# Four images through four fused layers: how far layer 0 of the next image runs ahead, and in which pool a second set of tiles lies

## The chip, the cores and the metric

The kernel runs on one core of one Trainium2 chip. Its time is device microseconds of one launch; the median of several runs is the metric. PE is TensorE, DVE is VectorE, ACT is ScalarE, POOL is GpSimd, SP is the engine that issues most DMAs. Each engine takes its instructions in the order of its own queue; semaphores order them across engines.

## The reference

Four images of 32×32 pixels and 384 channels in float32 go through four residual layers, each on a group-normalized input:

```python
x = x + _L0_conv_ref(_gn(x), ...)   # deformable attention, 6 heads of 64
x = x + _L1_conv_ref(_gn(x), ...)   # attention, 12 heads of 32, weighted by a group similarity
x = x + _L2_conv_ref(_gn(x))        # box sums over 5 pixels and 20 channels, quotient
x = x + _L3_conv_ref(_gn(x), ...)   # 3x3 outlook attention
```

Layer 0 makes queries `q`, a grouped 3×3 convolution of them, LayerNorm, GELU and a tanh offset per pixel and group. At the offset positions it samples the image bilinearly (a gather), makes keys and values from the samples, samples a table of relative biases for each pair of pixels, and takes a softmax over 1024 keys:

```python
attn = jnp.einsum('bmhc,bnhc->bhmn', qh, k) * scale
attn = jax.nn.softmax(attn + bias, axis=-1)
out = jnp.einsum('bhmn,bnhc->bmhc', attn, v)
```

Layer 1 takes `softmax(q k)`, multiplies it by a group weight, and normalizes over the queries (`axis=2`) before it multiplies by the values:

```python
sim = jax.nn.sigmoid(sim_beta + sim_alpha * jnp.einsum('bhnd,bhmd->bhnm', _l2norm(xg_h), _l2norm(gc)))
group_weight = jnp.einsum('bhnm,bhkm->bhnk', sim, sim) * gamma + (1.0 - gamma)
attn = softmax(q k * scale) * group_weight
attn = attn / (attn.sum(axis=2, keepdims=True) + 1e-08)
out = jnp.einsum('bhnm,bhmd->bhnd', attn, v)
```

Images are independent of each other.

## The kernel before

There are two lanes. **Front** does layer 0 of an image; **Trunk** does layers 1, 2 and 3. Layer 0 of image 0 runs by itself first. After that, the trunk of image b has layer 0 of image b+1 beside it, and the trunk of the last image has nothing beside it. The lanes hand over through DRAM: layer 0 writes `x1[b % 2]`, the trunk reads it.

Both lanes are Python generators that yield a weight after each small step. `layer3` draws from them: it advances the trunk by one step, adds the step's weight over `TRUNK_STEPS` (1109) to `done`, and then draws steps of the fronts, each worth its weight over `FRONT_STEPS` (714), until `ahead` has reached `done + LEAD`. So LEAD is the share of an image by which layer 0 of the next images is ahead of even progress. The order of these calls gives the priority; the scheduler of the language then places the instructions on each engine's queue, where an instruction that could be ready earlier may be put ahead of its turn.

The front of one image has these parts, with their steps: in `inputs0`, norm and transposes (35), queries (15, L553), the grouped convolution (45, L572), transposes, LayerNorm (L601 to L623) and GELU (L627) (25), `positions` (20, L433 to L503), eight gathers with their weighing and turning (64, L640, L653 to L656, L667), keys and values (30, dense products L364 and L378, evacuated at L694 and L700); then 12 half-heads of 38 steps in `head0`; then `w_out` (18). A half-head is 512 queries of one head. For each of eight key tiles it gathers a window of the bias table (`win`, L722), interpolates it (`z` L734 and L735, `lg` L739 and L740), multiplies queries and keys (L743), adds (L744) and keeps a running maximum (L749). Then come the maximum's broadcast (L762), the exponentials (L775, L776) and the products with values and ones (L778).

The trunk of one image: `inputs1` (173 steps) has the norm, queries and keys of layer 1 (evacuated at L847 and L849), the gate's projection and its strided depthwise convolution (L881, L883), the inverse norms (`inv`, L912), values (L919), and the normalized gates (L930, L938, L944); the softmax sums of the first four heads go in between (`sums_step`, L1011 to L1024). Then six `pair`s of heads (118 steps each): similarities (`sims`, L1064 and L1071), and for eight key tiles the scaled similarity `sg` (POOL, L1126), logits (L1141), exponent (L1149), similarity product (L1171), the weighting with the sum over queries (L1180) and the products with the values (L1115). Last, `layers23` (228 steps): `out1` (L1219), the box sums (L1235 to L1282), and layer 3 (attention and values L1302 to L1316, convolution of the weights L1341, a skewed copy through DRAM L1375 and L1377, products L1387, output L1401).

Tiles lie in pools that are opened and closed by `scope`, the trunk's from the low end of SBUF, the front's from the high end. In the trunk, pool `l1` is open for the whole layer 1, `l1a` for `inputs1`, `l1b` for the pairs. In the front, `l0` is open for the whole layer, `l0a` for `inputs0`, `l0b` for the heads. `pair_tiles` makes two sets of queries and keys (`qks[0]`, `qks[1]`, two tiles of 4 KB per partition each) in `l1`, and fills their padding rows by memsets on POOL (L966, L967). Pair p uses set p % 2; `load_pair(0)` is called in `inputs1`, `load_pair(1)` in the first pair. By the built program, `l1a` ends at byte 141056 of a partition, and `l0b` begins at byte 140576.

Of the kernel before, what the change touches and what calls it, by code (L numbers as in the profile page):

```python
# [26 lines left out]
P = 128  # L27
NB, HW, C = 4, 32, 384
N = HW * HW
# [3 lines left out]
NH1, HD1 = 12, 32  # L33
# [25 lines left out]

TRUNK_STEPS, FRONT_STEPS, LEAD = 1109.0, 714.0, 0.1


def bc(ap, axis, n):
# [7 lines left out]
class Net:  # L73
# [190 lines left out]
    def layer1(self, b):  # L264
        self.stages = [self.trunk.layer1(b)]
# [547 lines left out]
class Trunk(Lane):  # L813
# [3 lines left out]
    def layer1(self, b):  # L817
        with self.scope("l1"):
            self.pair_tiles()
            with self.scope("l1a"):  # L820
                yield from self.inputs1(b)
            with self.scope("l1b"):
                self.load_groups(0)
                st = None
                for p in range(NH1 // 2):
                    if p % 2 == 0:
                        u = p // 2 + 1
                        st = self.sums_state() if u < NH1 // 4 else None
                        if st:
                            self.load_quad(u)  # L830
                    yield from self.pair(p, st)
# [121 lines left out]
    def pair_tiles(self):  # L953

        nc = self.nc
        self.qks = [[self.wt([P, N], f"{t}{i}") for t in ("qa", "ka")] for i in range(2)]
        self.xg, self.gc = self.wt([P, N], "xg"), self.wt([P, M1], "gc")  # L960

        self.q4, self.k4 = self.wt([P, N], "q4"), self.wt([P, N], "k4")
        for r in range(2):
            rest = slice(64 * r + HD1, 64 * r + 64)
            for qa, ka in self.qks:
                nc.gpsimd.memset(qa[rest, :], 0.0)  # L966
                nc.gpsimd.memset(ka[rest, :], 1.0)  # L967
            nc.gpsimd.memset(self.xg[rest, :], 0.0)
            nc.gpsimd.memset(self.gc[rest, :], 0.0)

    def load_quad(self, u):

        rows = slice(u * P, (u + 1) * P)
        for t, src in ((self.q4, self.qd), (self.k4, self.kd)):
            self.nc.sync.dma_start(t, src[rows, :])
# [512 lines left out]
```

## Time and profile before

| | us |
|---|---|
| median of 3 runs | 5136.31 |
| runs | 5131.72, 5136.31, 5164.89 |
| the profiled execution | 5153.4 |
| its span, first to last instruction | 5151.6 |

| stage, by the trunk's marks in the trace | image 1 | image 3 |
|---|---|---|
| inputs of layer 1 | 1925 to 2145 | 4310 to 4488 |
| six pairs | 2145 to 2885 | 4488 to 4958 |
| layers 2 and 3 | 2885 to 3139 | 4958 to 5151 |

Image 1 has layer 0 of image 2 beside it, image 3 has nothing. Layer 0 of image 0 takes the first 641 us by itself. The mean granted TensorE clock is 0.871. A busy time in a window is the union of the records of an engine[...].

### The profile page before, as it was taken

Reading aid. Unit: us, or ns where it says so; the run is one execution under the profiler, and the core shown is the slowest. Engines: PE = TensorE matmul, PEld = TensorE weight load, DVE = VectorE, ACT = ScalarE, POOL = GpSimd, SP = SyncE. Lnnn points to the kernel's source line nnn. Section 1 sums busy time; section 2 is a strip of 40 time slices with the busy share of each in tenths; the row PEclk is TensorE's granted clock in tenths of the full one; section 3 lists DMA queues with packets and bytes.
Section 4 is the critical chain, followed back from the end, with each engine's and each line's share of the span. In section 5 each row is a group of like instructions: output and inputs, shape, how many; then the busy total and the mean of one; then the engine's idle time right before and its main releaser. Section 6 shows DMA issues by size and latency. Waiting matters only on the chain.

```text
span 5151.6 us, 47071 instructions
## 1 busy us (share of the span) xinstructions
PE 4290.8 (83%) x15676; PEld 1844.1 (36%) x15676; DVE 3213.1 (62%) x5718; ACT 2406.5 (47%) x4346; POOL 1069.2 (21%) x994
## 2 busy tenths in 40 slices
PE   4466687899898788799999889799999978899976
PEld 2122242333343353233333344233334334243434
DVE  3478627577877725567777753667787772455544
ACT  2155424566755113466666312456675511566520
POOL 1523203211212301221222210321121230000011
PEclk7677786899999887799999889689999988799987
DMA  5323242311212142221112124231121213101011
GB/s 113 107 80 87 69 149 73 104 45 46 72 42 83 37 134 93 83 88 56 57 53 60 46 86 138 83 95 51 42 77 42 73 52 108 55 11 31 14 36 37
DMA packets 226578, 361.60 MB, mean 70 GB/s; under 512 B 115939, under 2 KB 163136, under 8 KB 226336
## 3 DMA queue, kind: packets, MB, share of 16 engines
q1 hardware_dynamic: 165448, 192.11, 12.2%
q0 software_dynamic: 39936, 145.53, 9.7%
q10 hardware_dynamic: 20952, 20.96, 1.6%
q8 instruction: 124, 2.03, 0.2%
q14 instruction: 118, 0.97, 0.1%
HBM read 280.59 MB, written 79.26 MB: 70 GB/s over the span
## 4 chain that ended last, share of the span: by engine, by line
PE 52%; DVE 23%; ACT 12%; issue 6%; DMA 4%; POOL 3%; another core or an unknown queue 0%; SPq 0%; ACTq 0%; DVEq 0%; POOLq 0%
PE bank L1171 11%; PE big L364 7%; PE bank L778 5%; PE big L1141 5%; ACT big L1024 4%; PE bank L378 4%; PE bank L743 3%; PE big L1011 3%; DVE nmax L1019 3%; DVE lg L744 2%; DVE e L1180 2%; PE bank L1115 2%; DVE rmax L749 2%; PE bank L318 2%; PE bank L1166 2%
## 5 line engine op out<-in xcount | busy, mean ns | idle before, releaser
L1180 DVE SCALAR_TENSOR_TENSOR e<-bank,gam,e 128x512 f32<-128x512 f32 x768 | 562.8, 748 | 558.5 <-ACT gn L1179 253.0
L1171 PE MATMUL bank<-sim,sg 128*128 128x512 f32 (+3 forms) x2304 | 856.5, 508 | 5.1 <-DVE e L1180 5.1
L1024 ACT ACTIVATE big<-big,nmax 128x512 f32<-128x512 f32 x768 | 508.6, 662 | 421.2 <-DVE nmax L1019 380.2
L722 POOL DMA_INDIRECT win<-strips,widx x384 | 418.4, 1090 | 979.6 <-DVE z L735 414.9
L1149 ACT ACTIVATE e<-big 128x1024 f32<-128x1024 f32 x384 | 378.5, 1021 | 372.4 <-PE big L1141 362.3
L1171 PEld LDWEIGHTS bank<-sim,sg 128*128 128x128 f32 x2304 | 407.3, 199 | 363.0 <-issue 287.1
L1019 DVE TENSOR_REDUCE nmax<-big 128x2 f32<-128x1024 f32 x384 | 459.4, 1219 | 122.1 <-PE big L1011 82.2
L1011 PE MATMUL big<-k,q 32*128 32x512 f32 x1536 | 403.6, 744 | 146.6 <-ACT big L1024 74.4
L1141 PE MATMUL big<-qa,ka 64*128 64x512 f32 x1536 | 418.1, 627 | 16.2 <-ACT big L1024 8.0
L1126 POOL TENSOR_SCALAR sg<-sim,gam 128x512 f32<-128x512 f32 x192 | 152.0, 795 | 1323.7 <-PE bank L1171 963.2
L778 PE MATMUL bank<-lg,va 128*64 128x512 f32 x768 | 382.7, 649 | 41.6 <-ACT lg L776 41.5
L743 PE MATMUL bank<-qpad,kz 128*128 128x512 f32 x768 | 390.7, 639 | 25.2 <-DVE e L1180 13.2
L778 PE MATMUL bank<-lg,ones 128*64 128x512 f32 x768 | 382.0, 648 | 0.0
L734 ACT ACTIVATE z<-win,bias_f 128x528 f32<-128x528 f32 x384 | 277.8, 738 | 202.0 <-DVE lg L740 119.3
L740 DVE SCALAR_TENSOR_TENSOR lg<-z,bias_f,lg 128x512 f32<-128x512 f32 x384 | 290.2, 767 | 64.2 <-ACT lg L739 61.6
L640 POOL DMA_INDIRECT gat<-pairs,sidx x192 | 206.4, 1075 | 583.1 <-DVE ix_fl L451 328.6
L735 DVE SCALAR_TENSOR_TENSOR z<-win,bias_f,z 128x528 f32<-128x528 f32 x384 | 292.9, 777 | 39.0 <-ACT z L734 27.5
L739 ACT ACTIVATE lg<-z,bias_f 128x512 f32<-128x512 f32 x384 | 270.4, 721 | 47.3 <-DVE z L735 34.3
L775 DVE TENSOR_TENSOR lg<-lg,tb 128x512 f32<-128x512 f32 x384 | 240.6, 686 | 77.2 <-ACT tb L768 77.2
L744 DVE TENSOR_TENSOR lg<-bank,lg 128x512 f32<-128x512 f32 x384 | 257.4, 684 | 47.0 <-PE bank L743 44.0
L776 ACT ACTIVATE lg<-lg 128x512 f32<-128x512 f32 x384 | 222.5, 629 | 39.2 <-DVE lg L775 38.8
L743 PEld LDWEIGHTS bank<-qpad,kz 128*128 128x128 f32 x768 | 138.9, 197 | 271.8 <-issue 141.3
(252 smaller groups left out, 6040.8 us busy)
## 6 DMA issues: line engine op xcount, KB each, us to landing
pairs<-xn SPq DMA_DIRECT2D x64, 192.0 KB
w<-in_gmat SPq DMA_DIRECT2D x16, 576.0 KB
w<-in_w_off SPq DMA_DIRECT2D x12, 576.0 KB
w<-in_Wqkv SPq DMA_DIRECT2D x12, 576.0 KB
a<-in_x SPq DMA_DIRECT2D x16, 384.0 KB
x<-a ACTq DMA_DIRECT2D x4, 1536.0 KB
k<-a SPq DMA_DIRECT2D x12, 512.0 KB
kz<-k SPq DMA_DIRECT2D x24, 256.0 KB
```

Source lines behind the costliest of these rows:

```text
L364: nc.tensor.matmul(ps[:, h * 512 : (h + 1) * 512], w[:, ki, lo + ko * P : lo + (ko + 1) * P], mov, start=ki == 0, stop=ki == KC - 1,)
L722: nc.gpsimd.indirect_dma_start(out=win, out_offset=None, in_=self.strips[:, :], in_offset=bass.IndirectOffsetOnAxis(ap=self.widx[:, q, c : ...
L743: nc.tensor.matmul(ps, kz[:, j * P : (j + 1) * P], both, start=True, stop=True)
L744: v.tensor_tensor(lf, ps, lf, ALU.add)
L778: nc.tensor.matmul(po[out, :], w, lf, start=j == 0, stop=j == NJ - 1)
L1011: nc.tensor.matmul(ps[c // 2][:, c % 2, :], self.q4[rows, i * P : (i + 1) * P], self.k4[rows, h * 512 : (h + 1) * 512], start=True, stop=True,
L1019: v.tensor_reduce(nmax[:, 2 * g : 2 * g + 2, i, h], ps[g], AX.X, ALU.max, negate=True)
L1024: nc.scalar.activation(ps[g][:, r, :], ps[g][:, r, :], AF.Exp, bias=nmax[:, c, i, h : h + 1], accum_out=den[:, c, i, h : h + 1],)
L1141: nc.tensor.matmul(ps[:, r, :], ka[rows, j * P : (j + 1) * P], qa[rows, cols], start=True, stop=True,)
L1149: nc.scalar.activation(e, ps, AF.Exp)
L1171: nc.tensor.matmul(ps[:, (mid - i0) * P :], sg[:, r, m, :], sim[:, r, m, mid * P : i1 * P], start=m == 0, stop=m == 1,)
L1180: v.scalar_tensor_tensor(e[:, r, :], ps, self.gam[:, 1:2], e[:, r, :], ALU.add, ALU.mult, accum_out=tot[:, r, h : h + 1],)
```

## The change

LEAD becomes 0.18, which is 57 front steps more. The second set of queries and keys is made at the start of the pairs, in pool `l1b`, and its four memsets are issued there; the first set stays in `l1`. Pool `l1a` then begins 8192 bytes lower and ends at byte 132864; `l1b` keeps its end. Lines after `load_groups(0)` move by 1, those after `pair_tiles` by 8. No arithmetic is added or removed.

```diff
-TRUNK_STEPS, FRONT_STEPS, LEAD = 1109.0, 714.0, 0.1
+TRUNK_STEPS, FRONT_STEPS, LEAD = 1109.0, 714.0, 0.18
...
                 self.load_groups(0)
+                self.pair_set()
                 st = None
...
-        self.qks = [[self.wt([P, N], f"{t}{i}") for t in ("qa", "ka")] for i in range(2)]
+        self.qks = []
+        self.pair_set()
         self.xg, self.gc = self.wt([P, N], "xg"), self.wt([P, M1], "gc")
...
-            for qa, ka in self.qks:
-                nc.gpsimd.memset(qa[rest, :], 0.0)
-                nc.gpsimd.memset(ka[rest, :], 1.0)
             nc.gpsimd.memset(self.xg[rest, :], 0.0)
             nc.gpsimd.memset(self.gc[rest, :], 0.0)
+
+    def pair_set(self):
+
+        qa, ka = [self.wt([P, N], f"{t}{len(self.qks)}") for t in ("qa", "ka")]
+        for r in range(2):
+            rest = slice(64 * r + HD1, 64 * r + 64)
+            self.nc.gpsimd.memset(qa[rest, :], 0.0)
+            self.nc.gpsimd.memset(ka[rest, :], 1.0)
+        self.qks.append((qa, ka))
```

## The prediction

> **What bounds the kernel now.** I first read the busy shares, then cut the span at the trunk's own marks (its first query evacuation, first `sims`, first `out1`) and asked for the busy time of each engine in each piece. Image 1 with layer 0 of image 2 beside it is the first three rows below; image 3, which has nothing beside it, the last three. Columns: stretch, length, busy PE, weight loads, DVE, ACT, POOL, then the granted PE clock, DMA share, GB/s.
>
> ```profile
> PE 4290.8 (83%) x15676; PEld 1844.1 (36%) x15676; DVE 3213.1 (62%) x5718; ACT 2406.5 (47%) x4346; POOL 1069.2 (21%) x994
> ...
> 1925.00:2145.00 220.00, 169.03 (x455) 68.13 (x447) 128.42 (x198) 83.79 (x184) 61.04 (x66) 0.72 0.31 99
> 2145.00:2885.00 740.00, 690.90 (x2675) 280.97 (x2676) 542.05 (x1066) 469.55 (x829) 151.99 (x154) 0.97 0.21 61
> 2885.00:3139.00 254.00, 208.05 (x782) 107.78 (x784) 126.91 (x164) 47.20 (x75) 51.90 (x24) 0.83 0.29 88
> 4310.00:4488.00 178.00, 143.79 (x363) 58.26 (x363) 75.89 (x92) 70.31 (x158) 10.00 (x18) 0.77 0.24 84
> 4488.00:4958.00 470.00, 450.08 (x2029) 194.33 (x2028) 244.93 (x602) 285.53 (x523) 33.20 (x48) 0.99 0.07 21
> 4958.00:5151.00 193.00, 119.37 (x376) 70.57 (x376) 91.85 (x101) 15.88 (x23) 44.38 (x19) 0.74 0.13 40
> ```
>
> The reader is to see three kinds of stage. The pairs (740 us) are TensorE's: 691 of 740 busy at clock 0.97. The inputs of layer 1 (220) are a chain of short waits: PE shows 169 busy, but at 0.72, and DVE 128. The tail, layers 2 and 3 (254), lies between. Beside layer 0 they cost 42, 270 and 61 us more than alone. So the question is which part of layer 0 lies beside which stage. The chain that ended last, cut to the end of the inputs and the start of the pairs (start, length, what):
>
> ```profile
> 2068.64 8.15 DVE inv L912
> ...
> 2097.48 9.24 PE bank L378 x24
> ...
> 2116.23 1.75 DVE gat L653
> ...
> 2136.98 3.79 PE big L930 x4
> ...
> 2176.75 15.45 PE big L364 x36
> 2192.20 15.49 PE bank L378 x48
> 2208.44 4.65 DMA win<-strips,widx
> ```
>
> Two things are to be seen. The end of the inputs waits for DVE, layer 0's weighing (L653) among it; and the keys and values of layer 0 (15.45 + 15.49 = 30.9 us of unbroken PE) stand on the chain inside the pairs, where PE is short, followed by a 4.65 us window gather.
>
> **What the Trainium skill says.** "TensorE: Matmul & The Clock Gate", Part 1, has an idle PE fall to half clock and warm up under load. The trace agrees in kind: 0.72 to 0.77 in the gappy stages, 0.97 to 0.99 in the pairs. So "PE busy" overstates the work in the inputs. The same page (the section on the array of 32×32) calls ACT and DVE strict FIFOs; the trace fits it, since a trunk instruction never passes a front instruction ahead of it. "ScalarE: Activation LUTs", What ACT_TABLE_LOAD costs, gives about 1283 ns for a table load; this trace has 1283 ns for each of its 109.
>
> **The change, part by part.** *The lead.* 0.08 of 714 steps is 57 steps; each stage of the trunk now has a later part of layer 0 beside it. By the built programs' order on each engine:
> - inputs of layer 1: before, third convolution, LayerNorm, GELU, positions, five of eight gathers; after, all eight gathers, keys and values, and 16 `z`, 13 `lg` of head 0.
> - pairs: before, three gathers, keys and values, then 10.5 half-heads; after, 12 half-heads without those first 16 and 13.
> - tail: before, 1.5 half-heads, `w_out`, then norm, transposes, queries, two convolutions; after, `w_out`, then all of that, the third convolution, LayerNorm, GELU and positions.
>
> *Pairs, each of three.* PE at full clock: a half-head is 16 query-key records at 15.45/36 = 0.43 us (6.9), 32 value records (7.0 in the chain's rows of L778) and about 1.7 of transposes and the ones-matmul (estimated from the same 0.43), 15.6 in all. 12 less two tiles is 185; before, 10.5 half-heads and three more query-key tiles, 30.9 and some 2 of turns make 200. So PE gives back 15. DVE: the moved `z` and `lg` (16×0.777 + 13×0.767 = 22.4), keys and values (3×1.28 + 8×0.56 = 8.3) and three weighings (3×3.3) leave, 1.5 half-heads of some 14 each in exponent and maximum work come: about -20. ACT gives back 7, and four of its table loads per image (109 become 93 in all), 5 us. The stage's full-clock PE sum is about 625 by the same rates (an estimate: 200 for layer 0 and 425 for the trunk, which alone shows 450 busy), so 740×15/625 = 18; I take 17. 3×17 = 51.
>
> *Inputs.* PE gains 30.9 and 1.7 of query-key, loses 8 of convolution. DVE loses LayerNorm and positions (16 + 22, as the first image alone spends them between 87.7 and 127.9 us) and gains 10 + 8 + 22: even. The first 110 us of the stage, 91 alone, should save about 10, since weighing (8×3.3 = 26) replaces 39. The end, from L912 on, should lose: the kv block stands on PE ahead of L930, then the first window gather (4.65) and 16 `z` stand on DVE among L938 and L944. It lasts 68 us now, at a PE clock of 0.55 to 0.61 in the windows from 2068 to 2145; I take 83. Sum +5 for images 1 and 2. Image 0, where LayerNorm and positions stand in the opening burst before the trunk's first key evacuation (L849), gets +10: some 15 for the 16 us of LayerNorm less part of the same saving. Together +20. Bounds: -15 per image if kv fits in the idle PE, +30 if all of it is exposed.
>
> *Tail.* PE loses 14, DVE gains 23, but where it is free: after L1316 the trunk uses 6 us of DVE in 54. Convolutions move ahead of L1341 (16 us where there were about 10 of other work: +4), the heads leave the DVE-bound box sums. I take -10 for images 0 and 1, where the bounds are -25 and +15. For image 2 only `w_out` is left beside 213 us that are 193 alone: -9. Sum -29.
>
> *Edges.* The last image alone stays 841 us. Layer 0 of image 0 stays.
>
> *The second set.* Its four memsets (0.945 us each, 3.8) move to the start of the pairs, behind 20 window gathers in POOL's order and ahead of `sg`; its loads stand behind them on SP, and only the next pair needs them. Cover: `load_groups` and `sims` (four ACT evacuations of 1.2). Zero; at worst 4 per image. What it gives: the input pool ended at byte 141056 of a partition, the heads' pool of layer 0 begins at 140576; now it ends at 132864, so heads may start before the inputs end without a wait.
>
> Sum: -51 + 20 - 29 = -60 on the profiled execution's own 5153.4 us, 1.2%. The median of the runs, 5136.31, is 17 lower; the same share of it gives 5136.3×(1 - 60/5153) = 5076.5.
>
> **Rivals.** *No gain:* the kv block and its gather are exposed at the end of each inputs stage, +30 instead of +5 to +10, and the pairs keep their losses at boundaries. -51 + 90 - 29 = +10, near 5146; half of it gives 5111. For: L930 stands behind kv on an in-order PE. Against: at a clock of 0.55 to 0.61 PE is far from full in those 68 us. *Slower:* LayerNorm of the next image holds the trunk's outputs. All eight L1401 stand behind L623 on DVE, with positions' four 3.35 us instructions between them. If layer 0's convolutions come late, 16 + 5 (GELU) + 22 us fall in the path at both boundaries, and after the burst once more before L849: 3×43 = 129; with the forecast's -60, and 20 off that its sum already holds for image 0 and the convolutions, +49: 5185. It decides from the point at which L601 starts more than some 15 us after L1316's last. Against: the trunk waits there 11 us for its skewed rows' DMA anyway. *Not as it says:* no stage gains from its new neighbour, and only the loss of overlap is left. 640 (layer 0 alone) + 841 - 1214 = 267 us are saved per overlapped image; 0.08 of it is 21 us lost at the edges. That is contained in the edges above, and alone gives 5157.
>
> **How the numbers follow.** Forecast 0.55, no gain 0.22, loss of overlap only 0.08, slower 0.15. The forecast's own range is 5015 to 5110: three inputs at -15 to +15, tails at -25 to 0. Within 1% is about what a measurement of this kernel can tell from no change: below 5085 counts as faster. The forecast lies mostly there, so faster 0.54; same 0.3; slower 0.16. The range for 8 in 10 is 5015 to 5170, leaving the larger half of the slower case out.
>
> **What would show it.** Right: pairs with layer 0 beside them at 720 to 726, inputs at 220 to 235 with more PE and a higher clock, tails 240 to 250, last image 841. Wrong: L930 waiting for L364 or `win` for over 20 us, L1401 ending later after L1316, `sg` waiting for the memsets of `qa`, or pairs that stay at 740, which would say that PE's sum is not what sets them.

## The result, and the profile after

The changed kernel takes 5153.93 us in the median of 10 runs (5144.38 to 5157.43). The kernel before, beside it on the same chip, takes 5141.27 in the median of 10. The ratio is 1.0019, 95% interval 1.0004 to 1.0033: no difference of 1% in either direction, where a gain of 1.2% was forecast. The profiled run took 5157.4 us with a span of 5155.6.

The gain was made and given back within each image. The table cuts both profiled executions at the trunk's own marks: from the last output of the image before to the first query evacuation ("gap", for image 0 the opening norm), from there to the end of `inv`, from there to the start of the first evacuation of `sims`, then the pairs, up to the evacuation of the sixth one's output, and the tail. Microseconds, before → after:

| | gap | to `inv` | end of inputs | pairs | tail | sum |
|---|---|---|---|---|---|---|
| image 0 | 92 → 96 | 119 → 139 | 70 → 93 | 739 → 728 | 257 → 233 | 1277 → 1289 |
| image 1 | 34 → 43 | 119 → 107 | 72 → 95 | 736 → 730 | 254 → 234 | 1215 → 1209 |
| image 2 | 34 → 39 | 119 → 107 | 71 → 94 | 734 → 727 | 213 → 199 | 1171 → 1166 |
| image 3 | 30 → 30 | 100 → 100 | 53 → 53 | 466 → 465 | 191 → 192 | 840 → 840 |

Stages with the same work in them differ by up to 5 us within one execution (67, 70 and 72 us for the end of the inputs in the kernel with seven parts and lead 0.10, below), so a single difference of that size says little.

The page's busy line of the kernel after, and its table by windows. The columns are stretch, length, busy PE, weight loads, DVE, ACT, POOL, granted PE clock, DMA share and GB/s. The first row is image 0 up to `inv`; the others are image 1, stage by stage.

```profile
PE 4253.8 (83%) x15676; PEld 1825.4 (35%) x15676; DVE 3239.3 (63%) x5718; ACT 2383.3 (46%) x4330; POOL 1082.6 (21%) x994
...
743.00:883.00 140.00, 95.76 (x242) 37.32 (x241) 98.91 (x143) 52.48 (x107) 51.98 (x48) 0.72 0.30 97
...
1937.00:1980.00 43.00, 15.87 (x47) 11.26 (x48) 17.72 (x61) 1.62 (x3) 24.17 (x32) 0.52 0.35 110
1980.00:2087.00 107.00, 93.24 (x242) 36.41 (x241) 69.70 (x73) 46.59 (x97) 35.48 (x30) 0.79 0.32 104
2087.00:2182.00 95.00, 81.71 (x193) 33.56 (x192) 53.21 (x70) 45.18 (x99) 23.09 (x22) 0.74 0.47 153
2182.00:2912.00 730.00, 680.05 (x2669) 268.43 (x2667) 536.62 (x1056) 459.50 (x816) 137.32 (x139) 0.98 0.18 50
2912.00:3146.00 234.00, 183.13 (x772) 100.39 (x772) 129.53 (x170) 40.30 (x69) 48.77 (x22) 0.85 0.33 98
```

The same cuts in the kernel before, at the marks of the table: image 0 to `inv`, image 1 to `inv`, the end of image 1's inputs, and its pairs.

```profile
738.00:857.00 119.00, 91.73 (x239) 35.11 (x237) 79.51 (x137) 52.24 (x108) 17.87 (x18) 0.80 0.26 86
...
1958.00:2077.00 119.00, 90.84 (x239) 35.13 (x237) 80.08 (x138) 52.27 (x108) 17.22 (x18) 0.81 0.26 86
2077.00:2149.00 72.00, 52.85 (x118) 20.07 (x118) 44.53 (x47) 30.26 (x75) 33.81 (x30) 0.59 0.38 121
2149.00:2885.00 736.00, 690.62 (x2674) 280.87 (x2675) 538.78 (x1063) 468.00 (x827) 151.99 (x154) 0.97 0.21 62
```

Three things are to be seen. The end of the inputs has 28.9 us more of PE in it (52.85 to 81.71, 75 more matmul records) and is 23 us longer. In the pairs PE lost 10.6 us against image 1 of before (690.6 to 680.1), and the stage only 6. And image 0 up to `inv` has 19 us more of DVE and 34 more of POOL than before, where image 1 has 10 less of DVE.

What stands on the path at the end of the inputs is in the chain of waits after, image 2 from `inv` to the first `sims` (start, length, what):

```profile
3283.89 8.15 DVE inv L913
...
3296.27 15.72 PE big L364 x36
3311.99 12.27 PE bank L378 x38
...
3324.99 4.93 DMA win<-strips,widx
...
3330.25 0.75 ACT z L734
...
3331.02 0.78 DVE z L735
...
3354.86 3.81 DMA win<-strips,widx
...
3374.72 3.78 PE big L931 x4
3378.50 3.71 PE big L1072 x6
```

The keys and values of layer 0 (L364, L378) are an unbroken 28 us of PE that begins 4 us after `inv`. The first window gather follows, and then `z` of the next image stands in line with the trunk's gates (L931 is L930 of before) until `sims` (L1072).

How much of the 23 us is the block's is read from the gates' first matmul. In image 1 of before, L930 first runs 16 us after `inv`, and the first `sims` are evacuated 56 us later. In the changed kernel L931 first runs 41 us after `inv`, and 54 us remain. So the stretch ahead of the gates grew by 25 us, and what follows them did not shrink by more than 2. The changed kernel, image 1, cut at the first L931:

```profile
2087.00:2128.00 41.00, 40.65 (x120) 20.78 (x120) 12.91 (x17) 7.28 (x18) 4.69 (x5) 1.00 0.37 124
2128.00:2182.00 54.00, 41.06 (x77) 12.78 (x72) 40.30 (x54) 37.90 (x82) 18.40 (x18) 0.53 0.54 175
```

The tail has a line that matters too. This is the chain in it, at the end of image 1:

```profile
3101.40 4.42 PE bank L1349 x36
...
3110.06 5.50 DMA skew<-urow
...
3118.36 0.87 DVE a L612 x2
...
3128.99 1.48 DVE y L1409 x3
...
3134.67 3.26 DVE ix_th L434
...
3142.04 3.34 DVE ix_th L434
3145.38 0.46 DVE y L1409
```

LayerNorm of image 2 (L612 to L623) and its positions (L433, L434) do stand ahead of and between the trunk's outputs (L1409 is L1401 of before), as the slower rival had it. The last output waits for the last L434: its input is ready 7 us before it starts. Yet the tail is 20 us shorter than before. Two half-heads have left it (64 records of L778 before, none after), while it now holds all 216 records of the convolutions, where it held 156.

### The profile page after: what moved, and what is told of

It is laid out like the page before. It is cut to its first block, busy times and chain, and to the rows that moved or that the text cites. A ratio compares the mean times of both kernels' runs of the same rounds, so it can differ in the third digit from the quotient of the medians.

```text
span 5155.6 us, 47074 instructions
## 1 busy us (share of the span) xinstructions
PE 4253.8 (83%) x15676; PEld 1825.4 (35%) x15676; DVE 3239.3 (63%) x5718; ACT 2383.3 (46%) x4330; POOL 1082.6 (21%) x994
## 5 line engine op out<-in xcount | busy, mean ns | idle before, releaser
L1179 PE MATMUL bank<-sim,sg 128*128 128x512 f32 (+3 forms) x2304 | 831.1, 496 | 2.5 <-DVE e L1188 2.5
L722 POOL DMA_INDIRECT win<-strips,widx x384 | 438.2, 1141 | 1265.6 <-DVE z L735 648.9
L778 PE MATMUL bank<-lg,va 128*64 128x512 f32 x768 | 381.7, 642 | 45.8 <-ACT lg L776 45.6
L743 PE MATMUL bank<-qpad,kz 128*128 128x512 f32 x768 | 391.3, 635 | 26.0 <-DVE e L1188 16.7
L778 PE MATMUL bank<-lg,ones 128*64 128x512 f32 x768 | 380.4, 641 | 0.0
L743 PEld LDWEIGHTS bank<-qpad,kz 128*128 128x128 f32 x768 | 136.4, 195 | 275.2 <-issue 143.4
L1149 PEld LDWEIGHTS big<-qa,ka 64*128 64x128 f32 x1536 | 136.1, 191 | 275.6 <-issue 147.7
```

Of the source, the lines that this page charges most:

```text
L722: nc.gpsimd.indirect_dma_start(out=win, out_offset=None, in_=self.strips[:, :], in_offset=bass.IndirectOffsetOnAxis(ap=self.widx[:, q, c : ...
L743: nc.tensor.matmul(ps, kz[:, j * P : (j + 1) * P], both, start=True, stop=True)
L778: nc.tensor.matmul(po[out, :], w, lf, start=j == 0, stop=j == NJ - 1)
L1149: nc.tensor.matmul(ps[:, r, :], ka[rows, j * P : (j + 1) * P], qa[rows, cols], start=True, stop=True,)
L1179: nc.tensor.matmul(ps[:, (mid - i0) * P :], sg[:, r, m, :], sim[:, r, m, mid * P : i1 * P], start=m == 0, stop=m == 1,)
```

## The experiments

Kernels run together shared one chip with their own runs of the kernel before; the ratios are to those. Gap, to `inv`, end of inputs, pairs and tail are of image 1.

| kernel | us | ratio to before, 95% | image 1 by stage | image 0 |
|---|---|---|---|---|
| second set moved, lead 0.10 | 5122.02 | 0.9995 (0.9984 to 1.0006) | 33, 116, 66, 739, 257 | 1264 |
| lead 0.18 from done 0.15 on | 5127.56 | 1.0008 (0.9999 to 1.0017) | 33, 107, 94, 727, 237 | 1287 |
| first half-head held | 5165.12 | 1.0074 (1.0060 to 1.0088) | 33, 107, 87, 757, 232 | 1293 |
| block and half-head held | 5188.92 | 1.0116 (1.0101 to 1.0132) | 33, 107, 56, 786, 237 | 1299 |
| block in seven parts, 0.18 | 5107.60 | 0.9974 (0.9964 to 0.9983) | 31, 106, 76, 742, 237 | 1272 |
| lead falling over image 2 | 5134.48 | 1.0018 (1.0008 to 1.0029) | 31, 105, 94, 731, 234 | 1283 |
| lead 0.06 | 5222.06 | 1.0194 (1.0181 to 1.0208) | 34, 137, 58, 744, 263 | 1280 |
| lead 0.14 | 5248.60 | 1.0200 (1.0181 to 1.0219) | 47, 106, 108, 724, 270 | 1294 |
| lead 0.16 | 5125.10 | 0.9971 (0.9960 to 0.9982) | 34, 110, 100, 718, 241 | 1276 |
| lead 0.26 | 5272.68 | 1.0298 (1.0284 to 1.0312) | 31, 146, 76, 737, 257 | 1396 |
| seven parts, 0.10 | 5145.59 | 0.9992 (0.9979 to 1.0004) | 36, 120, 67, 735, 253 | 1272 |
| seven parts, 0.14 | 5259.23 | 1.0221 (1.0201 to 1.0240) | 47, 106, 84, 746, 269 | 1299 |
| seven parts, 0.16 | 5086.67 | 0.9885 (0.9867 to 0.9904) | 33, 110, 72, 730, 241 | 1260 |
| seven parts, 0.20 | 5188.47 | 1.0099 (1.0081 to 1.0116) | 32, 117, 85, 745, 232 | 1314 |

**The second set alone.** LEAD stays 0.1, all else as changed.

```diff
-TRUNK_STEPS, FRONT_STEPS, LEAD = 1109.0, 714.0, 0.18
+TRUNK_STEPS, FRONT_STEPS, LEAD = 1109.0, 714.0, 0.1
```

> The lead stays 0.1, only the second set of queries and keys is made at the start of the pairs. Theory A (gains in tails and pairs are given back in the inputs of layer 1): the set costs nothing, 5141 within 8 us, stages as before. Rival C (the set's memsets and loads at the start of the pairs cost what the lead gains): each set of pairs is 4 to 10 us longer, 5155 to 5180.

0.9995: at this lead the set costs nothing and gives nothing, so the result is the lead's. The lead alone, with both sets in `l1`, was not run: heads that start inside the inputs would need pools `l1a` (to byte 141056) and `l0b` (from byte 140576) open together.

**Image 0.** The changed kernel, but the extra 0.08 is asked for only after the opening burst.

```diff
-                while self.ahead < self.done + LEAD:
+                lead = 0.1 if self.done < 0.15 else LEAD
+                while self.ahead < self.done + lead:
```

> The changed kernel, but the lead is 0.1 until the inputs of image 0's layer 1 are done, and 0.18 from there. Theory A: image 0's opening and inputs, 324 us with the lead of 0.18 and 275 with 0.1, come back to 275 to 285; its pairs have to take up 57 more steps and last 735 to 750 instead of 728; the rest as in the changed kernel: 5105 to 5130. Rival B (the 0.08 of overlap is lost whatever the place): the 57 steps cost in the pairs what they cost at the opening, 5145 to 5160.

Image 0 reaches `inv` after 116 us again, but then spends 101 at the end of its inputs and 745 in the pairs: 1287 in all, as with the burst (1289 after, 1283 to 1299 in the other kernels here with 0.18 and the block whole). The time lies in the range of the first guess, but only because the kernel before takes 5124 on this chip; by the ratio nothing is gained. So the opening burst is not the cause by itself. Image 0 has 57 more steps of layer 0 beside it than before, and pays for them wherever they stand. Against the second set alone, on the same chip, this kernel's image 0 is 23 us longer, and images 1 and 2 are 12 and 11 shorter (1198.5 after 1210.7, 1156.4 after 1167.4): the change pays once what it then earns twice. The gaps of 43 and 39 us in the changed kernel's profile are 33 here, and 31 to 33 in every other kernel with 0.18, so nothing is built on them; what lengthens them in that profile is open.

**The first half-head held.** The first half-head's first `z` keeps its place in the program's order, and the fronts stop at 233 steps while the inputs run. By the trace, four windows and none of the 16 `z` are left ahead of the first `sims`.

```diff
+                goal = self.done + LEAD
+                if self.done % 1.0 < 0.158:
+                    goal = min(goal, self.done // 1.0 + 233.0 / FRONT_STEPS)
+                while self.ahead < goal:
...
+            t = nc.scalar.activation(z, wv[:, 0:HH, 0 : HW + 1], AF.Copy, scale=sc(1, 1))
+            if h == 0 and q == 0:
+                self.tc.keep_in_program_order(t)
```

> The changed kernel, but the first half-head of layer 0 is pinned behind the trunk's steps so that only 4 of its 16 early z stand ahead of the pairs; keys and values stay in the inputs. If the early z and lg on VectorE are what lengthens the end of the inputs (94 us instead of 70): it falls to 75 to 82 and the pairs gain back 3 to 8 us, 5125 to 5145. If keys and values on TensorE are: it stays at 86 to 94, the pairs get longer by some 5, 5155 to 5170.

**The block held too.** As above, with the limit at 203 steps and the first product of every L364 and L378 of the keys and values kept in program order, so that they fall into the first pair.

```diff
-                    goal = min(goal, self.done // 1.0 + 233.0 / FRONT_STEPS)
+                    goal = min(goal, self.done // 1.0 + 203.0 / FRONT_STEPS)
...
-            ps = self.dense_t(w, xsT, ko)
+            ps = self.dense_t(w, xsT, ko, pin=pin)
...
-            ps = self.dense_n(xsT, w, j)
+            ps = self.dense_n(xsT, w, j, pin=pin)
```

> The changed kernel, but keys and values of layer 0 are held until the similarities of the first pair, and the first half-head behind them, so that the inputs have only the gathers and their weighing beside them. Theory A: the end of the inputs falls from 94 to 58 to 68 us, the pairs grow from 728 to 745 to 755, since 31 us of TensorE come back into them; tails stay at 234: 5115 to 5140. Rival B: the pairs grow by all that the inputs lose, 5150 to 5165.

Image 1, end of inputs and first pair, by windows: the kernel with the half-head held, then with the block held too.

```profile
2078.00:2165.00 87.00, 77.85 (x188) 32.58 (x187) 31.72 (x37) 28.42 (x70) 5.18 (x6) 0.76 0.32 108
2165.00:2312.00 147.00, 136.74 (x479) 51.52 (x479) 116.90 (x216) 106.23 (x191) 41.74 (x44) 0.92 0.28 79
```

```profile
2092.00:2147.00 55.00, 44.16 (x100) 15.57 (x99) 23.09 (x26) 27.80 (x70) 1.34 (x2) 0.62 0.26 87
2147.00:2329.00 182.00, 170.02 (x564) 68.42 (x566) 125.77 (x227) 106.70 (x191) 46.18 (x48) 0.93 0.31 89
```

Holding the half-head takes 8 us off the end of the inputs (95 after, 87 here) and puts 19 on the first pair (128 after, 147 here), 27 on all six (730 to 757): the early `z` were worth more than they cost. Holding the block takes 32 off (87 to 55) and puts 35 on (147 to 182); this kernel is slower than both guesses had it. The block of some 31 us of PE costs about its own length on either side. The idle PE at the end of the inputs hides none of it while it comes in one piece.

**The block in seven parts.** Lead 0.18. The 30 steps are given out as 5 after each of the three `ko` and 4, 4, 4, 3 after every second `j`, so that the trunk's steps come between; sum and arithmetic are the same.

```diff
+            yield 5
...
-        yield 30
+            if j % 2:
+                yield 4 if j < 7 else 3
```

> The changed kernel, but layer 0's keys and values are given out in seven steps of 3 to 5 instead of one of 30, so that the trunk's steps come between; 5 early z stand ahead of the pairs instead of 16. If it is the unbroken block of 31 us on TensorE that lengthens the end of the inputs: 94 falls to 75 to 82, time 5110 to 5135 on a chip where the kernel before takes 5124. If it is the work itself: the inputs stay within 5 us of their sum, the pairs take the held z back, 5135 to 5160.

Windows of image 1 in it, end of inputs and pairs:

```profile
2056.00:2131.00 75.00, 67.12 (x193) 29.08 (x191) 35.87 (x45) 30.52 (x74) 5.63 (x7) 0.97 0.38 129
...
2131.00:2873.00 742.00, 689.65 (x2666) 271.15 (x2666) 553.42 (x1081) 473.98 (x841) 155.39 (x155) 0.96 0.19 55
```

As many matmul records as in the changed kernel (193) take 75 us instead of 95, at a granted clock of 0.97 instead of 0.74. With them 17.3 us less of DVE stand there (53.21 to 35.87), as 3 `z` come early and not 16; the pairs take 12 us of the 20 back. What is left is a gain of 0.26% against before, and of 0.45% against the changed kernel by the two ratios. The same cut at the gates' first matmul, which is L933 here, and the records of that matmul in the changed kernel and here (durations in ns, minimum, median, maximum):

```profile
2056.00:2094.00 38.00, 35.61 (x103) 16.24 (x102) 13.42 (x14) 12.27 (x32) 0.00 (x0) 1.00 0.32 108
2094.00:2131.00 37.00, 31.52 (x91) 12.84 (x91) 22.46 (x32) 18.25 (x42) 5.63 (x7) 0.95 0.44 150
...
L931 PE MATMUL big<-inv,hall x12: 1056/1056/1217, 2139.9 to 2173.2; 32*128 32x512 f32 x12
...
L933 PE MATMUL big<-inv,hall x12: 587/588/692, 2093.9 to 2121.2; 32*128 32x512 f32 x12
```

The gates begin only 3 us earlier than with the block whole (38 after 41). The other 17 us are saved behind them (54 to 37), although half of the value products, 24 records, now stand there. With the first half-head held this stretch took 47 us at a clock of 0.55, so the early `z` account for some 7 of the 17; the other 10 go with the clock, 0.95 instead of 0.53.

**The lead falls over image 2.** From 0.18 at the start of its pairs to some 0.03 at its end.

```diff
-                while self.ahead < self.done + LEAD:
+                lead = LEAD - max(0.0, self.done - 2.16) * 0.18
+                while self.ahead < self.done + lead:
```

> The changed kernel, but from the pairs of image 2 on the lead falls evenly from 0.18 to 0.03, so that the last layer 0 ends with image 2's tail and not before it. Theory D: the 107 steps move from image 2's pairs, full, into its tail, which lasts 199 us now and 233 with a next layer 0 beside it: pairs 727 to 700, tail 199 to 215, 5 to 15 us less than the changed kernel. If the tail pays all: the same as the changed kernel within 5 us.

Image 2's pairs fall from 727 to 692, its tail rises from 199 to 238. Two half-heads left the pairs (12 to 10 by their exponentials), 35/2 = 17.5 us each, and the tail paid 39. Nothing is free in image 2's tail: the ratio is that of the changed kernel (1.0018 after 1.0019), as the second guess had it.

**Leads far from 0.1 and 0.18.** Only the constant differs.

> The lead is 0.26. Theory D (each 0.08 of lead costs about 21 us once, since image 0's trunk gets 57 more steps of layer 0 beside it and image 2's trunk 57 fewer; the rest is how the parts fall beside each other): against 0.18 another 15 to 25 us for image 0 and none back in image 2, images 1 and 2 within 8 us of the changed kernel: 5145 to 5175. If the phases dominate and a longer lead helps: below 5125.

> The lead is 0.06, with the second set at the start of the pairs. Theory D: image 0 has 29 steps fewer than with 0.1, about 10 us less; images 1 and 2 within 8 us of the kernel before, where layer 0's first convolutions and norm now stand in the inputs: 5105 to 5125 where the kernel before takes 5124. If the lead pays for itself by its phases: 5130 to 5150.

Both came out slower than either guess. A lead of 0.26 costs 3%: image 0 spends 229 us to `inv` where 119 were needed before, and images 1 and 2 spend 143 to 146, since keys, values and the windows of the first half-heads now stand in the first part of the inputs. A lead of 0.06 costs 1.9%: LayerNorm and positions then run 90 to 130 us after the query evacuation, and `inv` comes at 137; three half-heads stay in the tail (263).

**Between them: 0.14, whole and in seven parts, and seven parts at 0.10.**

> The lead is 0.14, keys and values in one step: they stand in the inputs, with 6 early z, and LayerNorm and positions in the tail, as with 0.18. Against 0.18 there are 29 steps fewer in image 0 and more in image 2. If the steps cost the same wherever they lie beside the trunk: as the changed kernel, 5125 to 5140. If image 0's extra steps are paid and image 2's are free: image 0 some 10 us shorter than with 0.18, 5110 to 5125.

> The lead is 0.14, keys and values in seven steps. They fall into the first pair, with LayerNorm and positions in the tail: the end of the inputs 60 to 70 us with the gathers alone, the first pair 135 to 145, the tail 233 to 240, image 0 shorter than with 0.18 by some 10 us: 5085 to 5110. If the inputs cannot be relieved without the pairs paying it all: 5120 to 5135.

> The lead of before, 0.1, and keys and values of layer 0 given out in seven steps. They stay in the first pair here. If the gain of the split comes from TensorE's block before L930 in the inputs: nothing to gain, 5115 to 5130 where the kernel before takes 5123, first pair 128 to 134 as before. If an unbroken block of 31 us costs anywhere: the first pair falls from 132 to 115 to 122 and the time to 5085 to 5105.

At 0.10 the splitting alone gives nothing (0.9992), and the first pair takes 134 us as expected for that case: the block lies in the pairs there. 0.14 was expected to lie between its neighbours and is 2% slower than before, whole or split. The chain of the kernel with 0.14 (block whole) at the end of image 1 shows a part of the reason:

```profile
3166.04 9.04 PE big L572 x72
...
3194.03 0.44 DVE y L1409
...
3196.96 2.07 DVE a L612 x2
...
3213.36 3.26 DVE a L433
...
3223.48 3.31 DVE ix_th L434
...
3227.11 4.01 PE bank L318 x18
```

The third convolution (L572, 9 us) stands between the trunk's last products, and the outputs end 270 us after the pairs, 36 later than in the changed kernel. Most of that was lost earlier: the trunk's L1310 (L1302 of before) starts 170 us after the pairs, and 150 in the changed kernel; why was not followed up. Then LayerNorm and positions follow, 30 us from 3197 to 3227, and the trunk's next norm (its sums L318) waits behind them on DVE: a gap of 47 us where the kernels of the table with other leads have 31 to 36. In the changed kernel the same instructions end with the last output. This gap is the slower rival of the prediction; the lead of 0.14 has it, and those of 0.16 and 0.18 do not.

**0.16 in seven parts, 0.16 whole, 0.20 in seven parts.**

> The lead is 0.16, keys and values in seven steps, most of them in the inputs and no early z. Between 0.18 split (5108) and 0.14 split: 5090 to 5115. If the early z matter more than where keys and values lie: above 5115.

> The changed kernel with a lead of 0.16 and nothing else, so with the keys and values of layer 0 in one unbroken block. Theory (the phases decide: with 0.16 LayerNorm and positions of the next image end just ahead of the trunk's outputs, in image 0 no convolution is caught up beside the opening burst): first part of the inputs 110 (image 0: 120 to 124), tails 240 to 245 and 202, gap 33 as in the kernel with 0.16 and the block in seven parts; end of inputs 84 to 92 because the block is whole, first pair 10 shorter; ratio to before 0.991 to 0.995. Rival (the gain at 0.16 is the splitting of the block): end of inputs over 92, ratio 0.998 to 1.003. Second rival (0.16 whole falls out of phase as 0.14 did): gap 45 or tail 265, ratio over 1.01.

> The block of keys and values in seven parts and a lead of 0.20. Theory (phases, and the opening burst pays for each step caught up): image 0 to the end of L912 145 to 152 against 134 at 0.18 and 122 at 0.16, so image 0 1283 to 1295; images 1 and 2 within 8 us of those at 0.18 (1192, 1150), the tail 225 to 235, the end of inputs 75 to 85 because more of the first half-head stands in it; ratio 0.996 to 1.001. Rival (the more lead the better, the block being what cost): image 0 no longer than at 0.18, images 1 and 2 10 us shorter, ratio 0.990 to 0.994.

The first rows are the kernel with 0.16 in seven parts: image 0 to `inv`, then image 1's end of inputs, pairs and tail. The last fence is 0.16 with the block whole, end of inputs and pairs.

```profile
740.00:863.00 123.00, 92.54 (x234) 35.53 (x232) 93.35 (x138) 51.19 (x105) 50.67 (x48) 0.75 0.34 111
...
2047.00:2119.00 72.00, 64.94 (x176) 27.67 (x177) 35.20 (x39) 29.47 (x72) 1.72 (x2) 0.88 0.32 105
2119.00:2848.00 729.00, 677.82 (x2655) 264.38 (x2653) 548.78 (x1083) 483.64 (x844) 168.20 (x158) 0.98 0.21 59
2848.00:3089.00 241.00, 196.77 (x810) 105.64 (x810) 134.52 (x178) 47.17 (x80) 50.12 (x23) 0.85 0.32 95
```

```profile
2065.00:2165.00 100.00, 78.95 (x193) 33.42 (x193) 55.79 (x71) 46.35 (x100) 19.39 (x19) 0.74 0.42 134
2165.00:2883.00 718.00, 670.65 (x2636) 262.55 (x2637) 530.80 (x1051) 465.79 (x816) 145.22 (x141) 0.98 0.18 52
```

0.16 in seven parts is faster than both kernels, by 1.15% against before. The two parts of that are told apart by the whole block at 0.16: the lead gives 0.3%, the splitting the other 0.9%. The splitting takes 28 us off the end of the inputs (100 to 72) and gives 11 to 12 back in the pairs (718 to 729). It is not all cutting: by the trace, 15 early `z` and half of the value products also move from the end of the inputs to the pairs. Holding the early `z` alone made the kernel with 0.18 slower, so they are not what gains. I had expected 84 to 92 for the whole block, and the rival's 92 and more came out; but the rival's ratio of 0.998 and more did not. At 0.20 image 0 takes 162 us to `inv`, after 134 at 0.18 and 122 at 0.16, all in seven parts: what image 0 pays grows steeply with the lead. Images 1 and 2 were also 19 and 24 us longer than at 0.18, outside what was expected; 11 of image 1's 19 lie before `inv` (117 against 106), and what waits there was not followed up.

## Why the prediction was wrong

The forecast was -60 us; the table's rows sum to +1, and the span is 4.0 us longer.

- **Inputs of layer 1: forecast +20, measured +83** (gap, to `inv`, and end, images 0 to 2: 47 + 20 + 16). This is the step that failed. Of the 83, 14 lie in the gaps of images 1 and 2, which no other kernel with 0.18 shows. The first part of images 1 and 2 saved 12 each, as forecast (10). "It lasts 68 us now ... I take 83" was the bad term: the end went from 71 to 94, +23 and not +15. The reason against the full exposure was the low clock, "PE is far from full in those 68 us". The trace and the two held kernels show that as wrong. The gates' first matmul comes 41 us after `inv` instead of 16, and the 54 us behind it are as long as before, with `z` in place of weighing: the idle PE that the prediction counted on lies behind the block, where the block has no share in it. In the held kernels 32 us come off when the block goes, 35 come on where it lands. Given out in seven, 20 us of the 23 vanish (end of inputs 75), and 12 return in the pairs; most of the 20 are saved behind the gates' first matmul, with fewer early `z` and at a higher clock.
- **Image 0, in the same sum: forecast +10 in its inputs, measured +43** (119 to 139 before `inv`, 70 to 93 after it). Layer 0 of image 1 has no tail of an earlier image to stand beside. The 57 steps are extra there, and 34 us of work on POOL, the gathers' engine, come in ahead of `inv`. The 21 us of lost overlap, which the prediction worked out in a rival and then called "contained in the edges above", were in no term of the sum; against the second set alone image 0 pays 23. Image 0 as a whole is 12 us longer, after its own pairs and tail gave 35. Asking for the lead later left it at 1287.
- **Pairs: forecast -51, measured -24.** By the trace, 10 half-heads stood in image 1's pairs before (320 records of L778), not 10.5, with the query-key products of 11 (176 records of L743); 12 stand there after, less 6 such records. At the prediction's own rates PE then gives back 11 us and not 15, and its records did shrink by 10.6. So the form of the step, PE's sum with the block out and half-heads in, was right. At the prediction's 740/625, 11 us would be 13 of the stage; 6 to 11 were measured, and where the rest went is open. DVE gave back 2 us (538.8 to 536.6) where 20 were forecast: one weighing left the pairs and not three, and two half-heads came and not one and a half. The tapered lead prices a half-head at 17.5. So the change had little to win here: two half-heads in (31 to 35) for one block out (31 to 35) and the `z`, `lg` and a weighing.
- **Tail: forecast -29, measured -58** (24, 20, 14). Mis-sized to the good side. Two half-heads left, not the 1.5 of the prediction, and the tails of images 0 and 1 gained 20 to 24 rather than 10. The tapered kernel puts two half-heads into image 2's tail for 39 us. And the tail pays for LayerNorm and positions on its chain all the same.
- **Edges and second set: nothing, measured nothing.** The last image is 840 in both, the set alone 0.9995.

Of the rivals, *no gain* had the mechanism at the end of the inputs and its outcome, with other parts: inputs of +83 against its 90, pairs and tail that together gave 82 against its 80. Its +10 us is also the measured difference (0.19% of 5141). Only the end of the inputs is 23 of the 30 that it put there; image 0's 20 ahead of `inv` and 18 in the gaps, less the 24 saved in the first parts, are the rest. *Slower* has the order of instructions in the changed kernel, but LayerNorm and positions end there with the last output. Its decision point was wrong: L601 starts 22 us after the last L1316 (L1324 here), and 37 with lead 0.16, both past the "some 15 us" and without the loss; with 0.14 it is 66 to 69, and the loss is there. *Loss of overlap only* names a time near the result (5157), but its +21 us is twice the measured difference, and every stage moved. It is right for image 0 alone.

Of what would show it: pairs at 720 to 726 came as 727 to 730, inputs at 220 to 235 as 240 to 245 (224 to 225 before, by these marks), tails at 240 to 250 as 233. L931 did stand behind L364 and L378 for over 20 us, which was named as the sign of being wrong.

## What to carry to other kernels

Idle time of an engine in a stage of short waits is no room for an unbroken block that comes ahead of the stage's own work: charge its full length, or try it in parts, which here gave 0.45% at a lead of 0.18 and 0.9% at 0.16, and nothing at 0.10 and 0.14. Shifting one lane against another does not trade smoothly: what counts is which instructions of one lane fall just ahead of a wait of the other, and 0.14, 0.16 and 0.18 of an image gave +2.0%, -0.3% and +0.2%; so work out for each stage boundary what lands there, and try the neighbours. When a lead grows, charge the first pass by itself, since it has nothing behind it to hide in.

## What the runs showed that was not expected

The granted PE clock at the end of the inputs follows the order of almost the same work: 193 matmul records took 81.7 us of busy PE at 0.74 with the block whole and 67.1 at 0.97 with it in seven parts. The low clock is not the block's. It is 1.00 up to the gates' first matmul in both kernels; in the stretch behind, it is 0.53 with the block whole and 0.95 with the parts of it in between, and one and the same matmul of the gates takes 1056 ns there or 588. So the 20 us gained can't be put down to the fit of the parts into the waits alone; whether the parts raise the clock, or something else does, no run tells apart.
